# The entry of a local-attention layer: DMA issues in written order, two loads behind two scatters, a zeroing cut in half

## The chip, the cores and the metric

The kernel runs on one core of one Trainium2 chip. A core has a matrix engine (TensorE, PE in the profile; its weight loads are PEld), a vector engine (DVE), a scalar engine (ACT), a general engine (POOL) and a sync engine (SP) that does nothing here but issue DMAs. Each engine works through its own instructions in order and waits at semaphores for the others. The metric is the time of one execution on the device in microseconds (us); lower is better.

## The reference

The network has four layers on a batch of 8 images of 56 x 56 x 192, each applied as `x = x + layer(groupnorm(x))`. The change lies in the second layer (layer 1 in the code), an "outlook" attention: each position of a 28 x 28 grid predicts, from the mean of its four pixels, a 9 x 9 weighting of a 3 x 3 neighbourhood, and the weighted values are added back at the nine places.

```python
v = x @ Wv
patches = jnp.stack([vp[:, i:i + STRIDE * h:STRIDE, j:j + STRIDE * w:STRIDE, :] for i in range(K) for j in range(K)], axis=3)
pooled = x.reshape(Bn, h, STRIDE, w, STRIDE, C).mean(axis=(2, 4))
a = pooled.reshape(Bn, h * w, C) @ Wa + ba
a = jax.nn.softmax(a.reshape(Bn, h * w, HEADS, KK, KK) * SCALE, axis=-1)
out = jnp.einsum('bnhpq,bnqhd->bnphd', a, patches)
# the nine parts of out are added at their places in acc
return acc[:, PAD:PAD + Hn, PAD:PAD + Wn, :] @ Wp + bp
```

## The kernel before

The layer is cut into 28 units: four pairs of images, seven strips of eight rows each. A unit n goes through these steps; the names are those of functions in `layer1`, the L numbers those of the profile.

- `load(n)` (L985, its DMAs at L989): six DMAs bring x of the unit into one of six buffers. The sum x + layer(x) is formed in this buffer and stored from it by `finish` (L1179).
- `normalize(n)`: ACT scales x into one of two buffers xn (three L1033), POOL carries over a border row (L1030) and forms the means of 2 x 2 pixels (L1038, L1040).
- `patches(n)`: DVE, ACT and POOL copy nine shifted views into xc (L1059, L1057, L1055).
- `attention(n)` has two halves. `logits`: PE (L1074, L1078), then DVE adds the bias and takes the maximum (L1083, L1084), POOL subtracts it (L1085). `weights`: ACT exp (L1088), DVE sum and reciprocal (L1089, L1090), POOL's product aq (L1094), and a DMA of SP, called ad(n) in the following, that writes aq to memory (L1099).
- `spread(n)` (L1106, its DMAs at L1112): fourteen DMAs read ad back and scatter it into a block-diagonal matrix bd, of which there are two; they wait for ad(n) to have landed, and are 30 KB each. Only the diagonal blocks are written, so both bd are filled with zeros once at the entry (L1231 on POOL, L1240 and L1261 on DVE). SP issues all fourteen, but for units 0 and 1 SP and POOL issue seven each.
- `values(n)`: four steps on PE (L1126), each copied out by ACT (L1130). Logits, value steps and fold share two PSUM buffers "c", so the third value step needs the first one's copy to be done.
- `attend(n)`: 192 matmuls of bd with the values (L1155), copied by ACT to ys (L1164); POOL adds and keeps the border row (L1166, L1169).
- `fold(n)`: the output projection on PE (L1197 to L1208), added to x by DVE (L1220).

The opening is written out by hand: normalize and patches for units 0 and 1, logits and weights for both, spreads 0 and 1, normalize(2). Then the loop (L1271) runs over n with, in this order: load(n + 4), normalize(n + 3), patches(n + 2), attend(n), logits(n + 2), two value steps of n + 1, weights(n + 2), the two other value steps, spread(n + 2), fold(n). For n = 0 there are no value steps, since they were in the opening.

On PE, DVE, ACT and POOL the instructions stand in the order in which they are written (`manual_schedule`, L971). SP is not in this list: a scheduler orders its DMAs by its own estimate of when their data is ready and their buffers free, which may put a DMA far ahead of the place where it is written. Around the entry it issues, in this order: the x loads of units 1 to 3, wp and bp, norm fetches of later pairs, ad(0), two more norm fetches, two of the six DMAs of unit 4's load, spread(0), the rest of unit 4's load and half of unit 5's, ad(1), the rest of unit 5's load, spread(1), two norm fetches of the last pair, the weights W_vb and b_vb of the next layer (written at n = 20), ad(2), spread(2), ad(3), half of the stores of unit 0, spread(3), the other half, ad(4), unit 6's load, spread(4). [...]

Of the kernel before, what the change touches and what calls it, by code (L numbers as in the profile page):

```python
# [926 lines left out]
def layer1(cx, xin, xout, w, consts):  # L927
# [9 lines left out]
    tc, nc = cx.tc, cx.nc  # L937
# [5 lines left out]
    NG = 2 * NR  # L943
# [12 lines left out]
    with ExitStack() as es:  # L956
# [13 lines left out]
        E = mybir.EngineType  # L970
# [3 lines left out]
        def parts(x, p, t):  # L974

            cols = slice(t * SW, (t + 1) * SW)
            for i in range(2):
                d = 2 * p + i
                yield x[0:CP, i], d, (slice(None), 0, cols)
                yield x[CP:CA, i], d, (slice(0, CA - CP), 1, cols)  # L980
                yield x[sides[i], 2], d, (slice(CA - CP, None), 1, cols)
# [3 lines left out]
        def load(n, queue=nc.sync):  # L985
            if n < len(units):
                xs[n] = cx.tile(xp, [128, 3, SW], "x")
                for dst, d, at in parts(xs[n], *units[n]):
                    queue.dma_start(dst, xin[d][at])  # L989

        def fetch_norms(p, queue):
            norms[p] = cx.tile(cp, [128, 3, 2], f"norm{p}")
            for i in range(2):
                src = cx.norms[2 * p + i]
                queue.dma_start(norms[p][:, i, :], src[0:CA])
                queue.dma_start(norms[p][sides[i], 2, :], src[CA:])
# [24 lines left out]
        bds = [cx.tile(cp, [NP, 2 * NG, NCOL, HEADS, 3], f"bd{i}") for i in range(2)]  # L1021

        def normalize(n):

            p, t = units[n]
            x, xn = xs[n], xns[n % 2]
            if t == 0:
                nc.gpsimd.memset(xn[:, 0, :, 1, :], 0.0)
            else:
                nc.gpsimd.tensor_copy(xn[:, 0, :, 1, :], xns[(n - 1) % 2][:, NR, :, 1, :])  # L1030
            for j in range(3):
                s, o = norms[p][:, j, 0:1], norms[p][:, j, 1:2]
                nc.scalar.activation(  # L1033
                    xn[:, 1:, j, :, 1:], x[:, j].rearrange("p (y i x) -> p y i x", i=2, x=H),
                    AF.Identity, bias=o, scale=s,
                )
            rows = cx.tile(sp, [128, NR, 3, H], "rows")
            nc.gpsimd.tensor_tensor(rows, xn[:, 1:, :, 0, 1:], xn[:, 1:, :, 1, 1:], ALU.add)  # L1038
            pool4 = cx.tile(wk, [128, 3, NR, N], "pool")
            nc.gpsimd.tensor_tensor(  # L1040
                pool4.rearrange("p j y x -> p y j x"), rows[:, :, :, 0:H:2], rows[:, :, :, 1:H:2], ALU.add
            )
            return pool4.rearrange("p j y x -> p j (y x)")

        def patches(n):

            xn = xns[n % 2]
            xc = cx.tile(wk, [128, 3 * NR, 2, KK, NX], "xc")
            for q in range(KK):
                j, i = divmod(q, 3)  # L1050
                src = xn[:, (i + 1) // 2 : (i + 1) // 2 + NR, :, (i + 1) % 2, j : j + 2 * N - 1 : 2]
                src = src.rearrange("p y j (u x) -> p (y j) u x", u=2)
                dst = xc[:, :, :, q, :]
                if q in (3, 7):
                    nc.gpsimd.tensor_copy(dst, src)  # L1055
                elif q in (1, 5):
                    nc.scalar.copy(dst, src)  # L1057
                else:
                    nc.vector.tensor_copy(dst, src)  # L1059
            return xc  # L1060
# [45 lines left out]
        def spread(n, ad, queues=(nc.sync, nc.sync)):  # L1106

            av = ad.rearrange("i (g x) q f -> x q (i g) f", x=NX)
            bd = bds[n % 2].rearrange("p g c h i -> p g (c h i)")
            for x in range(NX):  # L1110
                at = 2 * x * 3 * HEADS
                queues[x % 2].dma_start(bd[x : x + (KK - 1) * NX + 1 : NX, :, at : at + HK], av[x])  # L1112
# [29 lines left out]
        def attend(n, v):  # L1142


            bd, t = bds[n % 2], units[n][1]
            py = cx.tile(psy, [128, 3, 512], "y")
            for g in range(NG):
                r, half = divmod(g, 2)
                i0 = int(t == 0 and r == 0)
                c0 = int(half == 0)  # L1150
                dims = (NCOL - c0, 3 - i0)
                to = (half * 2 * NX + c0 - 1) * NY + 2 * r + i0
                for k, block in enumerate(blocks):
                    for u, (i, h) in enumerate(block):
                        nc.tensor.matmul(  # L1155
                            sub(py[u * HD : (u + 1) * HD, k, to:], (NY, dims[0]), (1, dims[1])),
                            v[:, i, g, h * HD : (h + 1) * HD],
                            bd[:, i * NG + g, c0:, h, i0:],
                            start=(g == 0), stop=True, skip_group_check=True,
                        )  # L1160
            ys = cx.tile(sp, [128, 3, NY, H], "ys")
            lo = int(t == 0)
            src = py[:, :, 0 : NY * H].rearrange("p j (x y) -> p j y x", y=NY)
            nc.scalar.copy(ys[:, :, lo:, :], src[:, :, lo:, :])  # L1164
            if t:
                nc.gpsimd.tensor_tensor(ys[:, :, 0, :], ys[:, :, 0, :], carry.pop(0), ALU.add)  # L1166
            if t < NT - 1:
                carry[0] = cx.tile(sp, [128, 3, H], "carry", bufs=2)
                nc.gpsimd.tensor_copy(carry[0], ys[:, :, NY - 1, :])  # L1169
            return ys  # L1170
# [58 lines left out]
        for i, xn in enumerate(xns):  # L1229
            nc.gpsimd.memset(xn[:, :, :, :, 0], 0.0)  # L1230
        nc.gpsimd.memset(bds[0][:, 0:NG], 0.0)  # L1231
        pools[0] = normalize(0)
        xcs[0] = patches(0)
        warm = cx.tile(sp, [1, 1], "warm")
# [14 lines left out]
            f()  # L1249
        second = attention(pools.pop(1), ads)  # L1250
        second[0]()
        spread(0, ads.pop(0), (nc.sync, nc.gpsimd))
        vs[1] = cx.tile(wk, [NP, 2, NG, C], "v")
        todo = values(xcs.pop(1), vs[1])
# [3 lines left out]
        pools[2] = normalize(2)  # L1258
        for f in todo:
            f()  # L1260
        nc.vector.memset(bds[1], 0.0)  # L1261
        spread(1, ads.pop(), (nc.sync, nc.gpsimd))
        gn = cx.gn = GroupNormPairs(cx, cx.keep, w["gmat"])
        gn.place = psb, "b"
# [6 lines left out]
        for n in range(len(units)):  # L1271
            if n == 2:
                for f in cx.late:
                    f(lambda: cx.tile(psb, [128, 512], "b"))
                fetch_norms(NPAIR - 1, nc.sync)
            load(n + 4)
            if n == 20:
                for t, name in zip(cx.held, ("W_vb0", "W_vb1")):
                    nc.sync.dma_start(t, consts[f"l2_{name}"])
                nc.sync.dma_start(cx.held[2], consts["l2_b_vb"].partition_broadcast(128))  # L1280
                for i in range(2):
                    nc.sync.dma_start(gn.first[:, i, :], cx.norms[i][0:CA])
                    nc.sync.dma_start(gn.first[sides[i], 2, :], cx.norms[i][CA:])
            if n + 3 < len(units):
                pools[n + 3] = normalize(n + 3)
            if n + 2 < len(units):
                xcs[n + 2] = patches(n + 2)
            ys = attend(n, vs.pop(n))
            if n + 1 < len(units):
                todo = []  # L1290
                if n:
                    vs[n + 1] = cx.tile(wk, [NP, 2, NG, C], "v")
                    todo = values(xcs.pop(n + 1), vs[n + 1])
                if n + 2 < len(units):
                    logits, weights = attention(pools.pop(n + 2), ads)
                    logits()
                    todo.insert(2, weights)
                for f in todo:
                    f()
                if ads:  # L1300
                    spread(n + 2, ads.pop())
            if late and late[0][0] <= n:
                late.pop(0)[1]()
            fold(n, ys)
# [1043 lines left out]
def network(tc, d, out):  # L2348
    cx = Ctx(tc)
    B = d["x"].shape[0]  # L2350
    with ExitStack() as es:
        dp = es.enter_context(tc.tile_pool(name="mid", bufs=1, space=DRAM))
        ims = [[d["x"][b] for b in range(B)]]
        for n in range(3):
            ims.append([cx.tile(dp, [CP, 2, HW], f"x{n}_{b}") for b in range(B)])
        ims.append([out[b] for b in range(B)])
        for n, layer in enumerate((layer0, layer1, layer2, layer3)):
            w = {k[3:]: v for k, v in d.items() if k.startswith(f"l{n}_")}
            layer(cx, ims[n], ims[n + 1], w, d)
# [32 lines left out]
```

## Time and profile before

| | us |
|---|---|
| median of three runs (lowest, highest) | 3863.78 (3854.99, 3865.73) |
| the profiled execution, as timed | 3867.67 |
| its span, first to last instruction | 3865.6 |
| PE busy in it | 3706.9 |
| the layer's entry: attend(0), attend(1), attend(2), attend(3) begin on PE | 1847.74, 1864.42, 1893.39, 1915.33 |

Times inside the profile are counted from the start of the span. A line of a timeline gives start, duration, engine, source line, operation, what is written and read, how many such instructions follow each other, and in brackets how long the engine was idle before and what ended that. SPq, and other names with a q, are the issue of a DMA, not its transfer. A line of busy time by stage gives the stage, its length, then the busy time of PE, PEld, DVE, ACT and POOL, the share of the full clock granted to PE, the share of time that the DMA engines were busy, and their rate in GB/s.

### The profile page before, as it was taken

Reading aid. Unit: us, or ns where it says so; the run is one execution under the profiler, and the core shown is the slowest. Engines: PE = TensorE matmul, PEld = TensorE weight load, DVE = VectorE, ACT = ScalarE, POOL = GpSimd, SP = SyncE. Lnnn points to the kernel's source line nnn. Section 1 sums busy time; section 2 is a strip of 40 time slices with the busy share of each in tenths; the row PEclk is TensorE's granted clock in tenths of the full one; section 3 lists DMA queues with packets and bytes.
Section 4 is the critical chain, followed back from the end, with each engine's and each line's share of the span. In section 5 each row is a group of like instructions: output and inputs, shape, how many; then the busy total and the mean of one; then the engine's idle time right before and its main releaser. Section 6 shows DMA issues by size and latency. Waiting matters only on the chain. (4 is left out here: it accounts for less than half of the span.)

```text
span 3865.6 us, 116066 instructions
## 1 busy us (share of the span) xinstructions
PE 3706.9 (96%) x51036; PEld 2639.2 (68%) x51036; DVE 2421.6 (63%) x3267; ACT 1806.9 (47%) x2068; POOL 1535.1 (40%) x1336
## 2 busy tenths in 40 slices
PE   7999999999999999998899999899989999999998
PEld 5777878777777868777667666444435555556997
DVE  5657676665757677556444444665657777775665
ACT  4444455444445445344434433344335555554664
POOL 4232242323233242223433333333335545445776
PEclk9999999999999999999999999999999999999999
DMA  8866363434436263343344343656549767664333
GB/s 161 179 137 159 81 168 89 125 98 106 118 85 172 81 160 90 89 101 102 91 124 103 104 97 98 181 174 204 176 146 208 179 162 174 156 151 120 98 111 103
DMA packets 389502, 508.64 MB, mean 132 GB/s; under 512 B 175848, under 2 KB 325672, under 8 KB 387606
## 3 DMA queue, kind: packets, MB, share of 16 engines
q1 hardware_dynamic: 386502, 496.22, 50.0%
q8 instruction: 401, 6.57, 0.7%
q0 software_dynamic: 1424, 4.14, 0.4%
q10 hardware_dynamic: 1072, 0.87, 0.1%
q14 instruction: 103, 0.84, 0.1%
HBM read 345.38 MB, written 155.65 MB: 130 GB/s over the span
## 5 line engine op out<-in xcount | busy, mean ns | idle before, releaser
L438 POOL TENSOR_TENSOR qv<-s,s 128x392 f32<-128x392 f32 (+3 forms) x320 | 564.8, 1796 | 1171.6 <-ACT s L418 796.7
L410 PE MATMUL c<-x,wqv 64*128 64x392 f32 x2592 | 458.4, 497 | 8.4 <-ACT s L418 4.9
L410 PEld LDWEIGHTS c<-x,wqv 64*128 64x128 f32 x2592 | 244.9, 188 | 161.8 <-ACT s L418 6.2
L418 ACT ACTIVATE s<-c,bqv 128x784 f32<-128x784 f32 (+1 forms) x247 | 224.8, 913 | 223.0 <-PE c L410 214.5
L432 DVE TENSOR_TENSOR qv<-s,s 128x784 f32<-128x784 f32 (+1 forms) x160 | 258.9, 1634 | 98.8 <-ACT s L418 98.8
L552 PE MATMUL c<-x,wp 64*128 64x224 f32 x2688 | 282.9, 356 | 14.0 <-ACT s L559 6.8
L471 ACT COPY or<-c 56x1024 f32<-56x1024 f32 x183 | 183.7, 1008 | 222.1 <-DVE ol L471 220.2
L471 DVE COPY ol<-c 56x1024 f32<-56x1024 f32 x184 | 221.7, 1210 | 84.9 <-PE c L465 84.6
L552 PEld LDWEIGHTS c<-x,wp 64*128 64x128 f32 x2688 | 254.8, 189 | 18.7 <-ACT s L559 9.0
L576 DVE TENSOR_TENSOR s<-s,c 128x896 f32<-128x896 f32 x112 | 121.8, 1088 | 219.1 <-ACT s L559 212.8
L1126 PE MATMUL c<-wv,xc 128*126 128x192 f32 (+1 forms) x1792 | 248.9, 336 | 7.0 <-ACT v L1130 4.4
L1126 PEld LDWEIGHTS c<-wv,xc 128*126 128x126 f32 (+1 forms) x1792 | 218.1, 187 | 46.9 <-issue 36.9
L1686 ACT ACTIVATE vb<-sm 128x1024 f32<-128x1024 f32 (+1 forms) x100 | 103.7, 1040 | 258.1 <-issue 220.0
L559 ACT ACTIVATE s<-c,bp 128x448 f32<-128x448 f32 x224 | 129.9, 631 | 190.5 <-PE c L552 189.6
L1835 POOL TENSOR_TENSOR rs<-rs,sin_win 128x896 f32<-128x896 f32 x56 | 136.2, 2450 | 196.5 <-ACT rs L1824 196.5
L510 PEld LDWEIGHTS c<-or,ol 120*64 120x64 f32 (+1 forms) x6720 | 199.6, 133 | 21.4 <-issue 11.1
L510 PE MATMUL c<-or,ol 120*64 120x56 f32 (+1 forms) x6720 | 207.3, 221 | 6.6 <-ACT or L471 5.6
L2257 POOL TENSOR_TENSOR y<-y,s 128x448 f32<-128x448 f32 x164 | 181.4, 1106 | 79.5 <-ACT s L2227 74.7
L1675 PE MATMUL v<-wvb,wa 128*128 128x512 f32 (+1 forms) x400 | 193.2, 615 | 4.9 <-DVE wa L49 4.9
L2214 PE MATMUL h<-ringh,am 128*64 128x57 f32 (+1 forms) x4304 | 184.8, 232 | 7.8 <-DVE ringh L2220 6.1
L1913 ACT ACTIVATE us<-c,bub 128x896 f32<-128x896 f32 x84 | 84.6, 1008 | 222.1 <-PE c L1895 138.9
L1704 POOL TENSOR_TENSOR l<-vb,ta 128x512 f32<-128x512 f32 (+1 forms) x52 | 74.8, 1438 | 275.4 <-ACT vb L1686 275.4
(293 smaller groups left out, 7948.3 us busy)
## 6 DMA issues: line engine op xcount, KB each, us to landing
or<-tt SPq DMA_DIRECT2D x252, 196.0 KB
ol<-tt SPq DMA_DIRECT2D x252, 196.0 KB
vt<-v SPq DMA_DIRECT2D x56, 672.0 KB
v<-vb SPq DMA_DIRECT2D x96, 384.0 KB
x<-x SPq DMA_DIRECT2D x110, 168.0 KB
wqv<-in_l_w_qv SPq DMA_DIRECT2D x40, 384.0 KB
x<-in_x SPq DMA_DIRECT2D x64, 196.0 KB
x<-x SPq DMA_DIRECT2D x110, 112.0 KB
```

Source lines behind the costliest of these rows:

```text
L410: nc.tensor.matmul(ps[:, h, 0:n], wqv[q][rows, k, i, :], xn[rows, k, g * n : (g + 1) * n], start=(k == 0), stop=(k == 2),)
L418: nc.scalar.activation(t, ps[rows, :, 0:n], AF.Silu, bias=bqv[rows, j : j + 1])
L432: nc.vector.tensor_tensor(sub(qv[rows, 7 * g :, 64 + H - 1 :], (HH * 120, 2), (120, 7), (-1, H)), *(t.rearrange("p u (h w) -> p u h w", w= ...
L438: eng.tensor_tensor(sub(qv[rows, w0:, H - 1 - 7 * g - HH * u :], (120, w1 - w0), (-1, 7)), *(t[:, u].rearrange("p (h w) -> p w h", w=H)[:, ...
L471: copy(dst[:, :, :, i0 : i0 + 8], view[rows])
L510: nc.tensor.matmul(ps[u * 64 : u * 64 + m, k, v * H : (v + 1) * H], left[:, d * H : d * H + m], right[:, d * H : (d + 1) * H], start=True, ...
L552: nc.tensor.matmul(ps[:, h, u * n : (u + 1) * n], wps[j][rows, k, u, :], xn[rows, k, g * n : (g + 1) * n], start=(u == 0 and k == 0), stop ...
L1126: nc.tensor.matmul(out(i, u), group(2 if part else i, u)[rows], wv[part][rows], start=(first and u == 0), stop=True, skip_group_check=True,)
L1675: nc.tensor.matmul(out, x[:, at : at + n], wt, start=(k == 0), stop=(k == 1), skip_group_check=True,)
L1835: nc.gpsimd.tensor_tensor(view(b), view(b), tab[1], ALU.mult)
L2214: nc.tensor.matmul((pt if o == 2 else ps)[sides[c], y], am[a][:, o * CB : (o + 1) * CB], old[:, x], start=(m < 2 or (apart and m in (6, 7) ...
L2257: nc.gpsimd.tensor_tensor(v, v, line[0][:, j], ALU.add)
```

## The change

It has three parts, all in `layer1`. SP joins the engines that keep the written order, from the first normalize to the end of the loop's second turn (n = 1). The loads of units 4 and 5 are written behind spread(2) and spread(3), at the end of the turns n = 0 and n = 1; from n = 2 on the load stands where it stood. And the zeroing of the second bd, one DVE instruction of 126 x 8352 behind the last value step of unit 1, becomes two of 126 x 4176, of which one stands behind the maximum of the logits of unit 1 and the other in the old place.

```diff
         nc.gpsimd.memset(bds[0][:, 0:NG], 0.0)
+        opening = ExitStack()
+        opening.enter_context(tc.manual_schedule(engines={E.SP}))
         pools[0] = normalize(0)
...
         second[0]()
+        nc.vector.memset(bds[1][:, NG:], 0.0)
         spread(0, ads.pop(0), (nc.sync, nc.gpsimd))
...
-        nc.vector.memset(bds[1], 0.0)
+        nc.vector.memset(bds[1][:, 0:NG], 0.0)
         spread(1, ads.pop(), (nc.sync, nc.gpsimd))
...
-            load(n + 4)
+            if n > 1:
+                load(n + 4)
...
                 if ads:
                     spread(n + 2, ads.pop())
+                if n < 2:
+                    load(n + 4)
+                    if n == 1:
+                        opening.close()
```

In the built program SP's order becomes: the x loads of units 1 to 3, wp and bp as before; then two norm fetches of the last pair, W_vb and b_vb, which are written later, outside the ordered stretch; ad(0), spread(0), ad(1), spread(1), eight norm fetches, ad(2), spread(2), unit 4's load, ad(3), spread(3), unit 5's load, the stores of unit 0, unit 6's load, ad(4), spread(4). From there on it is the old order. PE, ACT and POOL keep theirs.

## The prediction

> **What bounds the kernel now.** I read the page first (which engine carries the span), then the chain of waits, then the timelines of SP, PE, ACT and POOL around 1811 to 1930 us, where the changed lines run, and last the busy time by stage.
>
> ```profile
> span 3865.6 us, 116066 instructions
> PE 3706.9 (96%) x51036; PEld 2639.2 (68%) x51036; DVE 2421.6 (63%) x3267; ACT 1806.9 (47%) x2068; POOL 1535.1 (40%) x1336
> ```
>
> PE is the bound as an average; only the 4% of the span in which it is idle can be won, but any new idle time of PE is added in full. The timeline says where it is idle at the entry (start, duration, what; idle before and its releaser in brackets):
>
> ```profile
> 1847.74 3.30 PE L1155 MATMUL y<-bd,v 126*32 126x56 f32 x144 [1.87 <-DMA x<-x]
> 1864.42 5.87 PE L1155 MATMUL y<-bd,v 126*32 126x84 f32 x192 [3.69 <-DMA bd<-ad]
> ...
> 1876.49 6.71 PE L1126 MATMUL c<-wv,xc 128*126 128x192 f32 x48 [1.23 <-DVE s L1083]
> ```
>
> The second line is attend(1), 3.69 us late because spread(1) landed late. SP shows why:
>
> ```profile
> 1836.48 0.53 SPq L1099 DMA_DIRECT2D ad<-aq  x1
> ...
> 1839.90 5.57 SPq L1112 DMA_DIRECT2D bd<-ad  x7
> 1845.51 6.38 SPq L989 DMA_DIRECT2D x<-x  x7
> 1852.00 0.52 SPq L1099 DMA_DIRECT2D ad<-aq  x1
> ...
> 1872.02 0.34 SPq L1099 DMA_DIRECT2D ad<-aq  x1
> 1875.12 11.14 SPq L1112 DMA_DIRECT2D bd<-ad  x14
> 1886.37 0.42 SPq L1099 DMA_DIRECT2D ad<-aq  x1
> ...
> 1889.89 11.49 SPq L1112 DMA_DIRECT2D bd<-ad  x14
> ...
> 1916.24 4.04 SPq L989 DMA_DIRECT2D x<-x  x6
> ```
>
> The second ad (1852.00) had its data from POOL at 1847.57 and stood 4.4 us behind x issues. But the same rows hold the price of the remedy: fourteen spread issues take 11.1 to 11.5 us of SP. ACT shows who needs those x loads:
>
> ```profile
> 1866.70 1.02 ACT L1088 ACTIVATE s<-s 112x972 f32<-112x972 f32 x1 [11.23 <-POOL s L1085]
> 1867.62 2.06 ACT L1033 ACTIVATE xn<-x,norm 128x448 f32<-128x448 f32 x3
> ...
> 1919.23 0.77 ACT L1033 ACTIVATE xn<-x,norm 128x448 f32<-128x448 f32 x1 [7.24 <-DMA x<-x]
> 1921.90 1.42 ACT L1033 ACTIVATE xn<-x,norm 128x448 f32<-128x448 f32 x2 [1.90 <-DMA x<-x]
> 1923.22 0.92 ACT L1057 COPY xc<-xn 128x336 f32<-128x336 f32 x2
> 1924.04 1.41 ACT L1164 COPY ys<-y 128x1512 f32<-128x1512 f32 x1
> 1925.35 0.79 ACT L1130 COPY v<-c 126x768 f32<-126x768 f32 x1
> ```
>
> At 1867.62 unit 4 is normalized with no wait: its x has long landed. The rows from 1919.23 are the template of a load that comes late (unit 6): ACT waits in its written order, and the v copies, for which PE's value steps wait, stand behind the normalization. From the first x issue (1916.24) to the end of the first v copy (1926.14) it took 9.9 us. After the entry nothing is slack:
>
> ```profile
> 1916.00:2000.00 84.00, 83.37 (x1214) 59.32 (x1208) 38.55 (x67) 33.89 (x45) 31.34 (x39) 1.00 0.45 119
> ```
>
> PE (first busy time) is busy 83.37 of 84 us, so what the entry loses stays lost.
>
> **The change part by part.** PE, ACT and POOL keep their order; DVE gets one instruction more; SP's order changes most. I write each step as a new time against the old one, and take T for the end of aq(2), 1871.99 before (1869.92 + 2.07).
>
> *The hoist.* In the built program, SP no longer issues six norm fetches (1833.27 to 1836.38) ahead of ad(0), but the fetch of pair 3's first norms, both W_vb and b_vb, which are written outside the ordered stretch and moved ahead by the scheduler. Before, they were issued behind spread(1), 1862.39 to 1865.00, 2.6 us, so ad(0) is issued about 0.5 us earlier, at 1835.95. But 3 x 256 KB now lie ahead of it. Before, these were moved in 1864 to 1868 at 197 GB/s (4 us, 788 KB) with 12 GB/s after, so hoisted to 1834.2 they are through by about 1839. Bounds for spread(0): -0.5 us if they do not disturb ad(0); +2.1 if ad(0)'s 425 KB come after them (1839 + 1.3 us at the 320 GB/s of the window 1814 to 1824, + 1.7 for its end to be told). I take +2.1, 1842.0, since rows of loaded DMA (ad(1), issue to spread, 4.5 us) are nearer than the idle one (ad(0), 3.4 us).
>
> *Spread(0) and attend(0).* Seven issues, 5.57 us, to 1847.6; PE began 2.27 us after the last one ended (1845.47 to 1847.74), so attend(0) begins at 1849.9. After an idle stretch of 4.0 us I give it the 5.87 us of the row after 3.69 us idle: 1855.8 (before: 1854.1).
>
> *ad(1) and spread(1).* POOL: spread(0) to 1842.0 + 4.29, then aq(1) 2.03: 1848.3. ad(1) is issued at once, no longer at 1852.0; with 3.9 us (mean of 3.4 and 4.5) spread(1) begins at 1852.3 and ends on POOL at 1856.5, not 1861.2. The 7.00 us wait of POOL nearly goes and PE's 3.69 with it: fold(0) ends at 1858.7 + 3.9 = 1862.6, after spread(1) has landed.
>
> *T.* Logits(2) end at 1855.8 + 2.9 = 1858.7, DVE's two 1861.2; POOL's share of normalize(3), patches(2) and the carry (1861.19 to 1864.82 before, 3.6 us) end at 1860.1; then sub 1.88, exp 1.02, den 2.0, aq 2.07, with 0.1 for hand-overs: T = 1868.3. **Gain: 3.7 us.**
>
> *Unit 4's load* now stands behind spread(2): ad(2) 3.1 us (1872.02 to 1875.12), spread 11.14 us, so its first issue is at 1868.3 + 14.4 = 1882.7. It was issued at 1838.5 before. ACT, behind exp(2), waits for it from about 1864 on; ys(1) and all v copies of unit 2 stand behind. With the template, the first v copy ends at 1882.7 + 9.9 = 1892.6. PE's third value step needs that copy (two c buffers); before it began at 1876.49 + 6.71/3 = 1878.7. **Loss up to here, the gain included: 13.9 us.**
>
> *Unit 5's load* stands behind spread(3) in the same way: second v copy 0.8, exp 1.0, den 2.0, aq 2.05: 1898.5; ad(3) 3.5 (1886.37 to 1889.89), spread 11.5, load and copies 9.9: 1923.4. Without this wait PE would get to that step of unit 3 at 1892.6 + 4.4 (two steps) + 1.4 (slow start after 17 us idle, as L1074's 3.27 us at 1820.41 against 1.88) + 23.6 (1883.2 to 1906.8 before) = 1922.0, so 1.4 us more are lost. Before it was 1906.8. **Sum: +16.6 us.**
>
> *Covered.* The zeroing: half of 7.02 us, 3.54 as L1240 shows, falls into DVE's 4.48 us of idle time after 1838.88; without that cover it would delay den(1) by up to 3.5 us. The other half ends by 1850.6, before ad(1) has landed. Norm fetches behind spread(1) are first read with unit 7. ACT's gmat fetch keeps its place. Unit 6's load now goes ahead of ad(4), which wins nothing: PE did not wait at that place.
>
> [...]
>
> **The rivals.**
> 1. *Not slower.* The load of unit 4 is hidden anyway, and only ad(1)'s gain remains: 3.7 us, and 1.3 for attend(1) at full clock, so about 3859 us. It decides if x4 can be issued by about 1865 (third step free at about 1875, less 9.9). For it: ACT does idle 11.23 us there today. Against: ad(2) itself is not issued before 1868, and SP takes its queue in order.
> 2. *Given back later.* The stages 2000 to 2400 leave PE idle 12.5 us. If the moved SP work shortened 8 of them, +8 us, 3872. Against: from unit 4 on the order is the old one.
> 3. *More than the sum.* The hoisted 0.77 MB and the gmat fetch hold up spread(0) as a whole, and ad(2), ad(3) take the 4.5 us of ad(1): +2 to 4, +2.4 and a slow start of 1.4 again: +23, 3887.
>
> **How the numbers follow.** The profiled execution took 3867.67 us, span 3865.6; the median of the runs is 3863.78, 3.9 below. The sum gives 3884.3 against the profiled one and 3880.4 against the median; I say 3880. Its own bounds: 12 (no disturbance by the hoist, -2.6; ad times at 3.05 us, -1; loads 0.5 faster each, -1) to 22. Chances: the forecast 0.68, rival 1 0.05, rival 2 0.12, rival 3 0.15. With the runs' own scatter (3854.99 to 3865.73) the range is 3869 to 3889. About 0.3%, 11.6 us, is what a measurement here can tell from no change: rival 3 and most of the forecast lie above it: slower 0.81, same 0.16, faster 0.03.
>
> **What would show it.** In the changed profile: the second ad within 1 us of aq(1); six x issues only after the fourteen of spread(2), again after spread(3); ACT's L1033 for unit 4 idle about 20 us "<- DMA x"; PE idle 15 to 18 us at L1126 of unit 2 "<- ACT v", and a little in unit 3; the 3.69 us before attend(1) gone. Wrong if unit 4's normalization waits for nothing, or if PE has gaps after unit 4 that close.

## The result, and the profile after

The changed kernel takes 3878.12 us (median of four runs, 3876.90 to 3881.16), the kernel before 3859.54 us (four runs, 3854.99 to 3865.73): a ratio of 1.0042, 95% interval 1.0028 to 1.0056, that is 16 us more (11 to 22); the two medians differ by 18.6. The prediction was 3880 us, slower. The profiled execution of the changed kernel took 3881.16 us, with a span of 3879.1.

The timelines below are of the changed kernel's entry. Times on this axis are 1.14 us earlier than in the profile of before: the last L709 matmuls ahead of the layer begin at 1810.20 instead of 1811.34. These are the rows, first of the kernel before, then of the changed one:

```profile
1811.34 0.84 PE L709 MATMUL o<-s,wo 64*64 64x392 f32 x8
```

```profile
1810.20 0.84 PE L709 MATMUL o<-s,wo 64*64 64x392 f32 x8
```

SP first (start, duration, what is issued):

```profile
1833.40 1.00 SPq L1283 DMA_DIRECT2D wvb<-in_l_W_vb  x2
...
1834.98 0.38 SPq L1099 DMA_DIRECT2D ad<-aq  x1
1839.96 5.58 SPq L1112 DMA_DIRECT2D bd<-ad  x7
1846.93 0.36 SPq L1099 DMA_DIRECT2D ad<-aq  x1
1850.19 5.41 SPq L1112 DMA_DIRECT2D bd<-ad  x7
...
1867.45 0.32 SPq L1099 DMA_DIRECT2D ad<-aq  x1
1870.54 11.24 SPq L1112 DMA_DIRECT2D bd<-ad  x14
1881.83 3.13 SPq L989 DMA_DIRECT2D x<-x  x6
1899.02 0.32 SPq L1099 DMA_DIRECT2D ad<-aq  x1
1902.17 11.37 SPq L1112 DMA_DIRECT2D bd<-ad  x14
1913.59 3.44 SPq L989 DMA_DIRECT2D x<-x  x6
```

No x issue stands between spread(0) and spread(1) any more, and ad(1) is issued at 1846.93, right behind aq(1), which POOL ends at 1846.90. The six issues of unit 4's load follow fourteen of spread(2) at 1881.83; before, the first of them was at 1838.50. Unit 5's follow spread(3).

ACT, in the same view, shows who waits for these loads:

```profile
1862.14 1.02 ACT L1088 ACTIVATE s<-s 112x972 f32<-112x972 f32 x1 [5.89 <-POOL s L1085]
1884.87 0.76 ACT L1033 ACTIVATE xn<-x,norm 128x448 f32<-128x448 f32 x1 [21.71 <-DMA x<-x]
...
1889.97 1.49 ACT L1130 COPY v<-c 126x768 f32<-126x768 f32 x2
1893.74 1.01 ACT L1088 ACTIVATE s<-s 112x972 f32<-112x972 f32 x1 [2.27 <-POOL s L1085]
...
1916.75 0.76 ACT L1033 ACTIVATE xn<-x,norm 128x448 f32<-128x448 f32 x1 [8.01 <-DMA x<-x]
...
1922.10 1.50 ACT L1130 COPY v<-c 126x768 f32<-126x768 f32 x2
```

Unit 4's normalization, which followed exp(2) without a wait before, now stands 21.71 us. All four v copies of unit 2 lie behind it in ACT's order (the x2 row at 1889.97 holds the first two), and PE's third value step needs the first:

```profile
1849.72 5.19 PE L1155 MATMUL y<-bd,v 126*32 126x56 f32 x192 [5.79 <-DMA ad<-aq]
...
1861.45 4.61 PE L1155 MATMUL y<-bd,v 126*32 126x84 f32 x192
...
1868.71 4.46 PE L1126 MATMUL c<-wv,xc 64*126 64x192 f32 x32
1890.82 7.48 PE L1126 MATMUL c<-wv,xc 64*126 64x192 f32 x32 [17.65 <-ACT v L1130]
...
1922.95 4.56 PE L1126 MATMUL c<-wv,xc 64*126 64x192 f32 x32 [1.04 <-ACT v L1130]
...
1932.17 4.59 PE L1155 MATMUL y<-bd,v 126*32 126x84 f32 x192
```

These are attend(0), attend(1), the value steps of unit 2 (two and two), the last two of unit 3, and attend(3). The 3.69 us ahead of attend(1) are gone. In their place PE is idle for 17.65 us in unit 2, works through the 32 matmuls behind that in 7.48 us where the same step of unit 3 takes 4.56, and is idle for 1.04 us in unit 3. In the profile of before unit 3 has no such wait; its value steps and attend(3):

```profile
1902.39 8.76 PE L1126 MATMUL c<-wv,xc 64*126 64x192 f32 x64
...
1915.33 4.54 PE L1155 MATMUL y<-bd,v 126*32 126x84 f32 x192
```

After attend(3) PE is as full as before (84 us from 2.17 us ahead of it; lengths and busy times of PE, PEld, DVE, ACT, POOL, then PE's granted clock):

```profile
1930.00:2014.00 84.00, 83.29 (x1128) 58.03 (x1128) 37.19 (x65) 33.25 (x43) 32.84 (x42) 1.00 0.41 106
```

So the difference was made before attend(3). Counted from the start of the last L709 row ahead of the layer, attend(3) begins at 103.99 us in the profile of before (1915.33 less 1811.34) and at 121.97 in the one of the changed kernel (1932.17 less 1810.20): 18.0 us. The whole spans differ by only 13.5; the rest of the program, 1950.3 and 1946.9 us after attend(3), accounts for 3.3 of that difference and the earlier start for 1.1, and both lie within what repeated runs scatter (10.7 us for the four of before).

### The profile page after: what moved, and what is told of

It reads as the page before. It is cut to its first block, busy times and chain, and to the rows that moved or that the text cites. A ratio compares the mean times of both kernels' runs of the same rounds, so it can differ in the third digit from the quotient of the medians.

```text
span 3879.1 us, 116066 instructions
## 1 busy us (share of the span) xinstructions
PE 3704.4 (95%) x51036; PEld 2637.1 (68%) x51036; DVE 2418.1 (62%) x3268; ACT 1807.4 (47%) x2068; POOL 1534.6 (40%) x1336
## 5 line engine op out<-in xcount | busy, mean ns | idle before, releaser
L510 PEld LDWEIGHTS c<-or,ol 120*64 120x64 f32 (+1 forms) x6720 | 200.7, 133 | 24.7 <-issue 14.6
```

The costliest lines, as they stand in the source:

```text
L510: nc.tensor.matmul(ps[u * 64 : u * 64 + m, k, v * H : (v + 1) * H], left[:, d * H : d * H + m], right[:, d * H : (d + 1) * H], start=True, ...
```

## The experiments

Twelve kernels, each timed in turn with the kernel before. The table gives the ratio to the kernel before with its 95% interval, and two readings of each profile: PE's idle time ahead of unit 2's third value step, put down to ACT's v, and the start of attend(3) after the start of the last L709 row. (Expectations that say "from the end of L709" count from this start, too.)

| kernel | ratio (interval) | wait in unit 2 | attend(3) |
|---|---|---|---|
| before | 1 | 0 | 103.99 |
| changed | 1.0042 (1.0028, 1.0056) | 17.65 | 121.97 |
| early loads | 0.9999 (0.9989, 1.0009) | 0 | 101.20 |
| loads moved, SP as before | 1.0003 (0.9993, 1.0014) | 0 | 104.94 |
| split zeroing only | 0.9998 (0.9988, 1.0007) | 0 | 104.33 |
| loads ahead of the spreads | 1.0014 (1.0005, 1.0023) | 4.97 | 107.39 |
| POOL issues half of spreads 2, 3 | 1.0030 (1.0021, 1.0038) | 11.78 | 114.47 |
| third load behind its spread | 1.0074 (1.0060, 1.0087) | 17.14 | 122.14 |
| weights later | 1.0040 (1.0025, 1.0055) | 18.44 | 121.47 |
| gmat later | 1.0051 (1.0037, 1.0064) | 17.28 | 121.58 |
| early loads, weights later | 0.9997 (0.9988, 1.0006) | 3.44 | 104.67 |
| early loads, gmat later | 0.9990 (0.9981, 0.9999) | 0 | 96.59 |
| the same again | 0.9987 (0.9978, 0.9996) | 0 | 98.07 |
| early loads, gmat later, weights behind unit 4's x | 0.9990 (0.9981, 0.9999) | 1.23 | 99.70 |

Where two rows have the same instructions on every engine, attend(3) differs by 1 to 1.5 us (103.99 and 104.94; 96.59 and 98.07): that is what one profile can tell.

**Which part of the change costs.** The theory: the two loads behind the long spreads. The rivals: SP's written order as such, with the weights that it lets slip ahead of ad(0); or the zeroing. First the changed kernel with both loads at the head of their turn, and SP's written order and the split zeroing kept:

```diff
-            if n > 1:
-                load(n + 4)
+            load(n + 4)
...
-                if n < 2:
-                    load(n + 4)
-                    if n == 1:
-                        opening.close()
+                if n == 1:
+                    opening.close()
```

> The changed kernel with the loads of units 4 and 5 back at the head of their turns, ahead of ad(2) and ad(3); SP in written order and the split zeroing stay. Theory (the late loads make the whole loss): ACT normalizes unit 4 without a wait, the 17.65 us gap of PE in unit 2 and the 1.04 us gap in unit 3 are gone, and the earlier ad(1) remains as a gain: about 4 us faster than the kernel before, ratio 0.998 to 1.000. Rival (the hoisted W_vb and b_vb or the written order itself makes the loss): still 8 us or more slower than before, ratio above 1.002.

Measured: 0.9999, and attend(3) at 101.20. The timeline of PE with early loads:

```profile
1847.85 5.51 PE L1155 MATMUL y<-bd,v 126*32 126x56 f32 x192 [5.34 <-DMA ad<-aq]
...
1859.90 4.35 PE L1155 MATMUL y<-bd,v 126*32 126x84 f32 x180
...
1870.87 6.71 PE L1126 MATMUL c<-wv,xc 128*126 128x192 f32 x48 [0.59 <-DVE s L1083]
```

attend(0) is as late as in the changed kernel, attend(1) has no wait, and the value steps of unit 2 run through but for 0.59 us. So the loss is the place of the two loads alone. What remains of the change wins some 3 us up to attend(3) (101.20 against 103.99 to 104.94), and this is less than the interval of the times, 4 us to each side, can show.

The loads alone, in the kernel before:

```diff
-            load(n + 4)
+            if n > 1:
+                load(n + 4)
...
                     spread(n + 2, ads.pop())
+                if n < 2:
+                    load(n + 4)
```

> Only the two loads are moved in the text, and SP is left to the scheduler as before: it puts every transfer where it stood, so this is the kernel before. All theories: ratio 1.000, within 0.001; what it shows beyond that is the scatter of a comparison. From the end of L709 to attend(3) 103 to 105 us.

Measured: 1.0003. The move in the text does nothing as long as SP is left to the scheduler; it takes the written order on SP to make it cost. The split zeroing alone:

```diff
         second[0]()
+        nc.vector.memset(bds[1][:, NG:], 0.0)
...
-        nc.vector.memset(bds[1], 0.0)
+        nc.vector.memset(bds[1][:, 0:NG], 0.0)
```

> Only the zeroing is split. My reading, that both halves lie in idle time of DVE: ratio 0.999 to 1.001, from the end of L709 to attend(3) 103 to 105 us (before: 103.99), den(1) no later than before. A theory in which the first half delays den(1): 3.5 us more and 1.001.

Measured: 0.9998, attend(3) at 104.33. The zeroing costs and wins nothing.

**Is it the issue time of the spreads?** If unit 4's load is late because fourteen issues stand ahead of it, the wait must shrink by the issues that are taken away, and come again wherever another load is put there. In the changed kernel 3.09 us pass from ad(2)'s issue to the first issue of spread(2), which waits for ad(2) to land; the fourteen issues take 11.24. First the loads between ad and spread:

```diff
+                if n < 2:
+                    load(n + 4)
                 if ads:
                     spread(n + 2, ads.pop())
-                if n < 2:
-                    load(n + 4)
-                    if n == 1:
-                        opening.close()
+                if n == 1:
+                    opening.close()
```

> The changed kernel with the two loads between ad and spread: behind ad(2) and ad(3), ahead of the fourteen issues of spread(2) and spread(3). Theory (it is the issue time of the fourteen that is paid): unit 4's load is issued 14 us earlier than in the changed kernel, PE's 17.65 us gap shrinks to about 3.6 us and the gap in unit 3 goes; ratio to before 0.999 to 1.001. Rival (the loads are late because of ad's own wait or slow transfers, not of the issue time): the gap stays above 10 us, ratio above 1.002.

Measured: 1.0014, just above what was expected. PE in this kernel:

```profile
1870.41 4.46 PE L1126 MATMUL c<-wv,xc 64*126 64x192 f32 x32
1879.85 7.02 PE L1126 MATMUL c<-wv,xc 64*126 64x192 f32 x32 [4.97 <-ACT v L1130]
```

The wait falls from 17.65 to 4.97 us, by 12.7. Unit 4's load now goes out 0.41 us after aq(2) instead of 14.41: it is rid of the fourteen issues and also of the wait for ad(2) to land, so this run does not tell the two apart. From its first issue to the end of the first v copy it takes 10.2 us here, 8.9 in the changed kernel. The slow start stays whole: 7.02 us for the 32 matmuls, as behind the long wait. Unit 5's load costs nothing here: PE runs the 64 matmuls of unit 3's value steps in one row of 8.76 us.

Then the order of the changed kernel, but with SP and POOL issuing seven each of spreads 2 and 3:

```diff
-                    spread(n + 2, ads.pop())
+                    spread(n + 2, ads.pop(), (nc.sync, nc.gpsimd if n < 2 else nc.sync))
```

> The changed kernel with POOL issuing seven of the fourteen DMAs of spread(2) and of spread(3), as it does for units 0 and 1; the order is unchanged. Theory: seven issues of SP less, 5.6 us, so unit 4's load goes out 5.6 us earlier and PE's gap in unit 2 falls from 17.65 to about 12 us; the gap in unit 3 goes; 6 to 7 us faster than the changed kernel, about 10 us slower than before, ratio 1.0025. Rival (transfers or landing times of the spread set the load's time): no change against the changed kernel, ratio 1.004.

Measured: 1.0030. SP, and PE, in this kernel:

```profile
1869.62 0.33 SPq L1099 DMA_DIRECT2D ad<-aq  x1
1872.79 5.49 SPq L1112 DMA_DIRECT2D bd<-ad  x7
1878.32 3.12 SPq L989 DMA_DIRECT2D x<-x  x6
```

```profile
1887.10 6.94 PE L1126 MATMUL c<-wv,xc 64*126 64x192 f32 x32 [11.78 <-ACT v L1130]
```

From ad(2) to unit 4's load SP now takes 8.70 us, not 14.38, and PE's wait falls by 5.87. ad(2) still takes 3.17 us, and the same data is moved: seven issues less are 5.7 us less. The wait in unit 3 is gone, as expected (its 64 matmuls stand in one row of 8.76 us), and attend(3) is 7.5 us earlier than in the changed kernel; the intervals of the two ratios overlap. And a third load, unit 6's, behind spread(4):

```diff
-            if n > 1:
+            if n > 2:
                 load(n + 4)
...
-                if n < 2:
+                if n < 3:
                     load(n + 4)
-                    if n == 1:
+                    if n == 2:
                         opening.close()
```

> The changed kernel, with unit 6's load behind spread(4) too. If a load behind fourteen spread issues costs what I say: the third value step of unit 4 waits some 10.6 us for ACT's v, and starts slowly (2.5 us) behind that; 13 us over the changed kernel, ratio to before 1.0075 (changed kernel: 1.0042). If only the first such load costs and a later one is hidden behind the time already lost: 1.004 to 1.005.

Measured: 1.0074, and a wait in unit 4 that was not there (PE's timeline, values of unit 4):

```profile
1936.63 4.46 PE L1126 MATMUL c<-wv,xc 64*126 64x192 f32 x32
1951.39 6.96 PE L1126 MATMUL c<-wv,xc 64*126 64x192 f32 x32 [10.30 <-ACT v L1130]
```

10.30 us and a slow start of 2.5 (6.96 less 4.46), as expected. attend(4) begins 155.23 us after the last L709 row, in the changed kernel 142.15: 13.1 us. Why the second such load (unit 5's) costs PE only 1.04 us in the changed kernel and the third 10.30 here is in PE's own rows. From one of these loads to the next the v copies come some 31 to 32 us apart. From the third value step of unit 2 to that of unit 3 PE has 31.1 us of its own to do in the changed kernel (1890.82 to 1921.91: the slow start, waits of 1.94 and 1.21 us at L131, an attend(2) of 6.66 us); from unit 3's to unit 4's it has 20.9 (1920.20 to 1941.09 here). With this the issue time of the spreads is shown as the greater part of the cause: one run halves it and one adds to it. The rest of the 14.4 us is the time for which the spread waits for ad(2).

**The weights ahead of ad(0), and gmat.** The prediction priced the weights at 2.1 us ahead of spread(0). In the changed kernel W_vb and b_vb behind spread(1) instead:

```diff
+        for t, name in zip(cx.held, ("W_vb0", "W_vb1")):
+            nc.sync.dma_start(t, consts[f"l2_{name}"])
+        nc.sync.dma_start(cx.held[2], consts["l2_b_vb"].partition_broadcast(128))
         for n in range(len(units)):
...
             if n == 20:
-                for t, name in zip(cx.held, ("W_vb0", "W_vb1")):
-                    nc.sync.dma_start(t, consts[f"l2_{name}"])
-                nc.sync.dma_start(cx.held[2], consts["l2_b_vb"].partition_broadcast(128))
```

> The changed kernel with W_vb and b_vb written into the ordered stretch behind spread(1), so that they no longer stand ahead of ad(0). Theory: the hoist costs some 3 us (spread(0) begins 2.5 us earlier on SP, POOL's share 0.9 us, aq(2) ends about 3 us earlier), and the two gaps of PE remain: about 13 us slower than before, ratio 1.0035. Rival (the hoist makes most of the loss): back to within 5 us of before, ratio below 1.0015.

Measured: 1.0040, no better than the changed kernel; aq(2) ends 0.7 us earlier, not 3. SP in this kernel:

```profile
1836.17 0.34 SPq L1099 DMA_DIRECT2D ad<-aq  x1
1839.52 5.58 SPq L1112 DMA_DIRECT2D bd<-ad  x7
1847.88 0.35 SPq L1099 DMA_DIRECT2D ad<-aq  x1
1852.75 5.39 SPq L1112 DMA_DIRECT2D bd<-ad  x7
```

ad(0) takes 3.35 us to spread(0), with the weights ahead of it 4.98: their price there is 1.6 us. But now ad(1) takes 4.87 instead of 3.26. Two chains meet in POOL's subtract of unit 2 (L1085): PE's attend(0) with the logits behind it, and POOL's own issue of spread(1) with the patches behind that. The first won 2.9 us, the second lost; the subtract begins 49.36 us after the last L709 row instead of 50.03. POOL in this kernel, and then in the changed one:

```profile
1853.28 4.18 POOL L1112 DMA_DIRECT2D bd<-ad  x7 [2.97 <-DMA ad<-aq]
...
1861.06 1.88 POOL L1085 TENSOR_TENSOR s<-s,top 112x972 f32<-112x972 f32 x1
```

```profile
1850.72 4.18 POOL L1112 DMA_DIRECT2D bd<-ad  x7 [1.41 <-DVE xc L1059]
...
1860.23 1.87 POOL L1085 TENSOR_TENSOR s<-s,top 112x972 f32<-112x972 f32 x1 [1.68 <-DVE top L1084]
```

In the first POOL comes late, and DVE's maximum has been done since 1858.74; in the second POOL waits for it.

What else lies there is the fetch of gmat, 576 KB, which ACT issues. In the changed kernel it falls among the last issues of spread(0): ACT issues it at 1843.98, SP's seven issues end at 1845.54. Attend(0) then begins 4.18 us after they end, in the profile of before, where gmat was issued at 1845.92 behind the last of them, 2.27. ACT's rows, before and then changed:

```profile
1845.92 0.33 ACTq L1339 DMA_DIRECT2D gmat<-in_l_gmat  x1
```

```profile
1843.98 0.33 ACTq L1347 DMA_DIRECT2D gmat<-in_l_gmat  x1
```

So gmat on SP, behind spread(1), in the changed kernel:

```diff
-        gn = cx.gn = GroupNormPairs(cx, cx.keep, w["gmat"])
+        gn = cx.gn = GroupNormPairs(cx, cx.keep, w["gmat"], nc.sync)
...
-        cx.nc.scalar.dma_start(self.g, gmat)
+        (queue or cx.nc.scalar).dma_start(self.g, gmat)
```

> The changed kernel, but the 576 KB gmat fetch goes on SP behind spread(1) instead of ACT among spread(0). If this fetch, and not the weights ahead of ad(0), holds attend(0) back: PE's 5.79 us of idle time before attend(0) fall to 2.5 to 3.5 us, while ad(0) still takes 5 us to spread(0). But sub(2) then waits for POOL, which issues spread(1) and makes the patches behind it, so of these 3 us at most 1.7 reach unit 4's load: from the end of L709 to attend(3) 120 to 122 us (changed kernel: 121.97; before: 103.99), ratio to before 1.0035 to 1.0045. If the hoisted weights hold attend(0) back, the idle time stays at 5.8 us.

Measured: 1.0051, above the 1.0035 to 1.0045 expected, though the interval reaches into that range. PE's idle time ahead of attend(0) is 3.94 us, more than the 2.5 to 3.5 expected, less than 5.79. In the five kernels with the weights ahead and gmat on ACT it is 4.74 to 6.27, in the three with gmat behind spread(1) 2.94 to 3.94 (two of these follow below). From ad(0) to attend(0) it is 14.6 to 15.6 us in the five, 12.85 to 12.98 in the three, and 11.5 to 11.7 in the three kernels with the weights behind spread(1). In weights later, one of these last, ACT still issues gmat, but at 1846.20, 1.1 us behind the end of SP's issues of spread(0), and attend(0) begins 11.67 us after ad(0), against 11.48 where gmat goes out behind spread(1). So the weights cost 1.4 us at attend(0) by themselves, and some 2 more because they push spread(0) beside the gmat fetch. The old program can show it, too: in the profile of "loads moved, SP as before" gmat happened to be issued at 1844.26, among spread(0)'s issues, and attend(0) began 15.2 us after ad(0), where the profile of before has 11.3; x loads lay there as well, and the profile names these as what ended the wait. But attend(3) is at 121.58, and the time is no better. This does not show that the 2 us are lost on the way: in this profile ad(0) was issued 1.7 us later on the axis than in the changed kernel, behind a later aq(0), so that attend(0) itself is no earlier (39.42 us against 39.52). The reason that the expectation gave did not come up: ahead of the subtract POOL waited 0.45 us for DVE's maximum.

The same question with early loads. Weights later, first:

> Loads of units 4 and 5 at the head of their loop step, SP in written order, W_vb and b_vb behind the norm fetches, i.e. behind spread(1). If the hoisted weights cost 3 us on the path: from the end of L709 to attend(3) 98 us (with the weights ahead: 101.20), ratio 0.999. If ad(1), then beside the gmat fetch, takes back what spread(0) wins (as in the kernel with late loads, where ad(1) took 4.87 in place of 3.26 us), and the weights now stand ahead of unit 4's x: 101 to 104 us, ratio 0.999 to 1.001.

Measured: 0.9997, attend(3) at 104.67: the second case, just above its 101 to 104. The weights now stand ahead of unit 4's x, PE waits 3.44 us for it in unit 2, and the slow start comes with it (7.49 us). Then gmat later, twice:

> Loads of units 4 and 5 at the head of their loop step, SP in written order, and the gmat fetch on SP behind spread(1). Unit 4's load now stands behind 576 KB more; ACT's wait for it, 2.14 us with the gmat fetch among spread(0), grows to 3 to 5 us, and PE's third value step has 2.4 us of slack there. From the end of L709 to attend(3) 99 to 103 us (loads back alone: 101.20), ratio to before 0.998 to 1.000. If the order of the entry's transfers were worth more than what the end of the entry takes, it would be below 0.998.

> The kernel with early loads and the gmat fetch behind spread(1) a second time, beside the variant. The first time: 0.9990, attend(3) 96.59 us after the last L709 row. If that was a gain: 0.9985 to 0.9995 again; if it was scatter: 0.9995 to 1.0005.

Measured: 0.9990 and 0.9987, both intervals below 1, attend(3) at 96.59 and 98.07, both earlier than the 99 to 103 expected. PE of the first, whole from attend(1) through the values of unit 2:

```profile
1843.32 5.31 PE L1155 MATMUL y<-bd,v 126*32 126x56 f32 x192 [2.94 <-DMA bd<-ad]
...
1855.16 5.05 PE L1155 MATMUL y<-bd,v 126*32 126x84 f32 x192
...
1862.86 8.76 PE L1126 MATMUL c<-wv,xc 64*126 64x192 f32 x64
```

This is 0.1% faster than the kernel before and, by the two ratios, 0.5% faster than the changed one: the change with its loads early and gmat behind spread(1). The entry is 6 to 8 us shorter than before. With early loads and gmat on ACT it was 3 us shorter; that the further 3 to 5 us come from gmat's place alone is not settled by two profiles that differ by 1.5 us between them. Last, the weights behind unit 4's x in this kernel:

```diff
             load(n + 4)
-            if n == 20:
+            if n == 0:
                 for t, name in zip(cx.held, ("W_vb0", "W_vb1")):
                     nc.sync.dma_start(t, consts[f"l2_{name}"])
                 nc.sync.dma_start(cx.held[2], consts["l2_b_vb"].partition_broadcast(128))
+            if n == 20:
```

> The kernel with early loads and the gmat fetch behind spread(1), and now W_vb and b_vb behind unit 4's load, so that neither lies among ad(0), spread(0) or ahead of x. This is the hoist's price by itself. If it is what the rows say: ad(0) to SP's first spread issue 3.4 us in place of 4.6, PE's idle time before attend(0) 1 to 2 us in place of 2.94, sub(2) 47 to 48 us after the last L709 row (48.09 with the weights ahead), attend(3) 95 to 97.5 us (96.59), ratio to before 0.998 to 0.9995. If the hoist were worth its 2 to 3 us in full: sub(2) at 45.5, attend(3) at 94.

Measured: 0.9990, the same as with the weights ahead. ad(0) takes 3.18 us to spread(0), PE's idle time ahead of attend(0) is 1.50, as expected; but the subtract of unit 2 begins at 48.48, where 48.09 and 49.54 were measured with the weights ahead, and attend(3) at 99.70, later than the expected 97.5. With gmat out of the way the hoist's price is 1.4 to 1.8 us at attend(0), and nothing at the end of the entry that these runs can see.

## Why the prediction was right, point by point

Its steps are compared on one axis, from the start of the last L709 row.

- *The hoist.* ad(0) was issued 0.4 us earlier (predicted 0.5), and spread(0) began 1.2 us later (predicted +2.1). Mis-sized by 0.9 us, between its two bounds. The 1.7 us "for its end to be told" in the upper bound was the author's estimate; no run shows it apart from the transfer: from ad(0)'s issue to the first of spread(0) it took 3.42 us before and 4.98 in the changed kernel.
- *attend(0).* 3.1 us later (39.52 against 36.40), predicted 2.2. The step that failed is "ACT's gmat fetch keeps its place". It did in ACT's order, but that place now lies among spread(0)'s issues. The rival that let gmat hold up spread(0) had the mechanism, though not the size of the whole.
- *ad(1) and attend(1).* ad(1) right behind aq(1), no wait ahead of attend(1): as predicted.
- *T, the end of aq(2).* 57.22 against 60.65, a gain of 3.4 us; predicted 3.7. That attend(0) began 0.9 us later than the steps have it was nearly made good by its length, 5.19 us in place of 5.87.
- *Unit 4's load.* First issue 14.41 us after aq(2) (1867.42 to 1881.83); predicted 14.4. From it to the end of the first v copy 8.9 us (two copies in 1.49 from 1889.97); the template said 9.9. Third value step 13.2 us later than before (80.62 against 67.39); predicted 13.9.
- *The slow start.* Predicted 1.4 us, from four matmuls of L1074; measured 2.9. This term was mis-sized most. Both are half the time for which PE was granted half the clock: some 2.8 us from L1074's start (a mean grant of 0.67 over the 4.3 us from 1820.41), 6.0 in unit 2 (0.60 over the 7.48 us from 1890.82). The forecast took the first length for the second.
- *exp(3).* Not in the prediction: ACT's exp waits 2.27 us for POOL's subtract, which stands behind POOL's half of normalize(4). POOL had waited for the same x. From the end of the first v copy to that of aq(3) it took 8.3 us, not 5.9. So unit 5's load was issued 1.2 us later than the steps say: these 2.4, less 0.7 by which unit 2's first v copy was early, less 0.4 of ad(3) and spread(3).
- *Unit 3.* PE waited 1.04 us; predicted 1.4. The slow start and exp(3) nearly cancel in this difference, since the one makes PE late and the other ACT. The step that both enter is 17.3 us later than before (112.75 against 95.43), where the sum said 16.6.
- *Nothing given back.* PE's stages after attend(3) are as full as before.

So the mechanism and its size came out: 16.6 us forecast, 16 us by the ratio, 18.0 us at attend(3) in one pair of profiles and 17.6 against the mean of three profiles of kernels with the old entry (103.99, 104.94, 104.33). Two sizes were wrong in opposite directions, template and slow start, and the 2.4 us that were overlooked at exp(3) reached PE only with its 1.04 us of unit 3, since the slow start had made PE late, too. That the sum came this near is in part luck. The other side, "not slower", is what the early loads show: had unit 4's x been issued in time, the change would have been within the noise.

## What to carry to other kernels

Here a load behind a burst of fourteen 30 KB DMAs on one queue was late by the issue time of the burst (11.24 us, 0.8 us each); put loads whose buffers are free ahead of the burst and of the DMA that the burst waits for (ahead of the burst alone, 4.97 us of the wait were left), or split the burst over two issuing engines (5.87 us less of the wait). An engine that is given the written order no longer brings forward what is written late, but what is written outside the ordered stretch can still slip into it (here W_vb and b_vb, ahead of ad(0)): compare the built order, transfer by transfer, with what runs beside it. And when two chains meet in one instruction, shortening one of them is worth only the distance to the other (2.9 us won on one were worth 0.7 here).

## What the runs showed that was not expected

The slow start of PE does not grow with the wait. Behind 18.44, 17.65, 17.28, 17.14, 11.78, 10.30, 4.97 and 3.44 us of idle time the 32 matmuls of two value steps took 6.90, 7.48, 6.04, 6.26, 6.94, 6.96, 7.02 and 7.49 us, behind 1.04 to 2.61 us 4.56 or 4.57 (five cases): 1.5 to 2.9 us more, in no order. Busy time by stage of the changed kernel, behind the long wait (the third figure from the end is the granted clock of PE):

```profile
1890.80:1894.50 3.70, 3.68 (x15) 3.24 (x16) 0.00 (x0) 1.43 (x2) 2.91 (x4) 0.50 0.00 0
1894.50:1898.30 3.80, 3.80 (x21) 3.57 (x21) 1.99 (x2) 1.05 (x2) 1.35 (x2) 0.69 0.00 0
```

Over the whole row of 7.48 us the mean grant is 0.60, that is half the clock for 6.0 us. In six of the eight rows (behind 17.65, 17.28, 11.78, 10.30, 4.97 and 3.44 us) the grants by stage give 3.1 to 6.1 us by the same working, and what is lost is about half of it. Between 2.61 us of idle time, behind which the row took 4.57 us, and 3.44 us, behind which it took 7.49 and was granted 0.50 for its first 3.7, the value steps change. Elsewhere in these runs less was enough. attend(2) in the profile of before stands behind two gaps of 1.95 and 1.21 us with eight short matmuls between them; the grant was 1.00 up to 1891.50, 0.50 from 1892.00 to 1898.00, thus for the first 4.6 us of attend(2), and 1.00 again from 1898.40:

```profile
1889.40 1.02 PE L131 MATMUL b<-mean,gmat 128*128 128x1 f32 x8 [1.95 <-DVE x L1220]
1891.62 1.83 PE L131 MATMUL b<-dev,gmat 128*128 128x1 f32 x8 [1.21 <-DVE dev L169]
1893.39 6.35 PE L1155 MATMUL y<-bd,v 126*32 126x84 f32 x192
```

attend(2) of the changed kernel, behind gaps of 1.94 and 1.21 us, was granted 0.50 for its first 5.4 us (1908.14 to 1913.50). Two further rows of 192 matmuls were slow behind a single gap: attend(0) of early loads, gmat later took 5.31 us behind 2.94 us of idle time, and attend(1) of split zeroing only 5.91 us behind 2.73, where attend(3) in the profile of before took 4.54 us at a granted 1.00. So on these runs the clock was halved behind gaps of less than 2 us, while 2.61 us left the value steps as fast as before; what decides is not shown.

With a 576 KB fetch by another engine beside a scatter of 30 KB pieces, what waits for the scatter began about 2 us later (14.6 to 15.6 us from ad(0) to attend(0) against 12.9), though in the changed kernel the fetch was issued after most of the pieces (1843.98; SP and POOL issue the pieces from 1839.96 to 1845.54). And of the fourteen issues of a spread, seven moved to POOL took 4.18 us there, beside 5.49 us on SP, in place of 11.24 us on SP alone.
